# Relative attention: softmax weights turned by 32x32 blocks on VectorE and regrouped through DRAM instead of transposed on TensorE

## The chip, the cores and the metric

The kernel runs on one core of a Trainium2 chip. The metric is the device time of one execution in microseconds. A core has a matrix engine (TensorE, PE in the profile; PEld are its weight loads), VectorE (DVE), ScalarE (ACT), GpSimd (POOL), and SyncE (SP), which here issues the DMAs. Each engine works through its own list of instructions in order and waits on semaphores for the others. Sixteen DMA engines move the data. All data here are float32.

## The reference, cut to what matters

The whole kernel is a sequence of four blocks (relative attention, six layers of local attention and feed-forward, causal attention, a mixture of experts), each followed by a layer norm. The change lies in the first block alone, for 16 batches of 256 tokens, 16 heads of width 8:

```python
q, k, v = (proj(Wq), proj(Wk), proj(Wv))          # [16, 16, 256, 8]
rel = jnp.clip(r[:, None] - r[None, :], -64, 64) + 64
a_q, a_k, a_v = Eq[rel], Ek[rel], Ev[rel]         # [256, 256, 8]
content = jnp.einsum('bhld,bhmd->bhlm', q, k)
rel_k = jnp.einsum('bhld,lmd->bhlm', q, a_k)
rel_q = jnp.einsum('bhmd,lmd->bhlm', k, a_q)
pos_pos = jnp.einsum('lmd,lmd->lm', a_q, a_k)
attn = softmax((content + rel_k + rel_q + pos_pos) / sqrt(8))
out = jnp.einsum('bhlm,bhmd->bhld', attn, v) + jnp.einsum('bhlm,lmd->bhld', attn, a_v)
```

Both products at the end sum over m, the key's position. TensorE sums over partitions, so the weights, which come out of the softmax with l on partitions, are needed with m on partitions.

## The kernel before, in words

**Units.** `relative_attention` treats one batch in eight units: u // 4 chooses the half lc of the queries (128 rows l), the rest of u a group of four heads. A unit is four heads by 128 rows by 256 columns. `weights` (L516) sums the logits in one big PSUM tile, with matmuls for the content and transposes that add the stored position terms `rk3` and `rkc3`; VectorE adds the other term `rq3`, writes the tile `r_lg` and reduces a bound `r_nb` (L558). `exponentials` (L570) makes the weights on ScalarE, in place in `r_lg`. `turn_weights` (L583) transposes the four heads in eight 128x128 transposes on TensorE (L593) into small PSUM tiles, and copies these to `r_pT` (ScalarE L597, VectorE L599), which has m on partitions.

**Use of pT.** When the four units of a half are there, `positions` (L601) multiplies `r_pT` with the relative values (L609, L622), and VectorE masks the result to `r_z` (L630). `values` (L637) multiplies `r_pT` with the projected values in `r_spread` (L645) and gathers `r_z` with `pick` (L656). `join`, `statistics` and `normalise` add the two parts, divide by the sum, add the residual and normalise.

**The position terms.** They are made per batch ahead of time. `turn` and `project` give q and k. `spread_k` (L344) and `shift` (L337) make operands on GpSimd. `rearranged` (L381) sends q or k through DRAM: GpSimd permutes into `r_perm` (L392), four DMAs on SP store it (`there`, L395), four more read it back as `spots` (`r_dk`, `r_dq`), each row to several partitions (`back`, L405, 128 KB each), and `diagonal` masks these on GpSimd (L417). `rq_half`, `rk_half` and the two `corners` steps multiply them with tables of the relative embeddings (L431, L456) and copy or add the results to `rq3` (ScalarE L470, L479), `rk3` (VectorE L490, with the term `pp`) and `rkc3` (VectorE L503).

**Order.** The table `TURNS` (L700) has eight turns for the eight units of a batch; one pass over it is called a batch slot here. An entry (n, step) does the step for the unit n units back, or, for steps that belong to a batch, for the batch n back; -1 is the batch to come. `run` (L771) emits them in this order, and `in_order` (L932) then holds every engine, SP's DMA issues among them, to the order of the program. So a step that waits holds up all that is behind it on its engine. Turn 1, for example, has the exponentials of the unit before, `rearranged` for k of the batch to come, `join`, and the weights of unit 1. Positions for the second half of a batch stand in turn 3 of the next slot, positions for the first half in turn 6.

**Buffers.** Big PSUM tiles: 2. Small ones: 4. `r_lg`: 3; `r_pT`: 2, one for each half.

Of the kernel before, what the change touches and what calls it, by code (L numbers as in the profile page):

```python
# [12 lines left out]
F32 = mybir.dt.float32  # L13
# [4 lines left out]
DRAM = bass.MemoryType.DRAM  # L18

P = 128  # L20
NB, S, D = 16, 256, 128
NT = S // P
H, HD = 16, 8
MAXD = 64
# [80 lines left out]
def bcast(ap, shape):  # L105
    return ap.to_broadcast(list(shape))
# [136 lines left out]
def relative_attention(tc, I, xb, env):  # L243
# [12 lines left out]
    nc = tc.nc  # L256
    V, A, G, T = nc.vector, nc.scalar, nc.gpsimd, nc.tensor
# [7 lines left out]
    with ExitStack() as ctx:  # L265
# [18 lines left out]
        tqc = [one.tile([P, P - 4], F32, name=f"r_tqc{k}") for k in range(2)]  # L284
        tkc = [one.tile([P, P - 4], F32, name=f"r_tkc{k}") for k in range(2)]
        held = ctx.enter_context(tc.tile_pool(name="r_rows", bufs=2, space=DRAM))

        pp = one.tile([P, P], F32, name="r_pp")
        ppc = one.tile([P, MAXD], F32, name="r_ppc")
# [19 lines left out]
        def of(three, b, lc):  # L309
            return three[lc * (1 + b % 2)]  # L310
# [44 lines left out]
        def project_v(b):  # L355

            ps = small()
            for t in range(NT):
                T.matmul(
                    ps[:, t * P : (t + 1) * P],  # L360
                    lhsT=st[b]["xT"][:, t * P : (t + 1) * P],
                    rhs=w["v"],
                    start=True,
                    stop=True,
                )
            v = spread
# [119 lines left out]
        def rk_half(b, s_):  # L486
            for t, l0, n, p_ in diagonals(tk, st[b]["d", "q"], s_):
                pc = pp[:, l0 : l0 + 4 * n].rearrange("p (g i) -> p g i", i=4).unsqueeze(2)
                o = of(rk3, b, t)[:, :, l0 : l0 + 4 * n]
                V.tensor_add(  # L490
                    o.rearrange("p h (g i) -> p g h i", i=4), p_, bcast(pc, (P, n, H, 4))
                )

        def rk_corners(b, phase):

# [14 lines left out]

        def heads(u):

            lc, ap, x = u // 4, u // 2 % 2, u % 2
            return lc, [8 * ap + 4 * k + 2 * x + j for k in range(2) for j in range(2)]

        def weights(b, u):  # L516
# [1 line left out]
            lc, hs = heads(u)  # L518
            s_ = st[b]
            if u % 4 == 0:  # L520
                st[b, lc] = {"den": two.tile([P, H], F32, name="r_den")}
# [24 lines left out]
            for j, h in enumerate(hs):  # L546
# [5 lines left out]
                    start=False,  # L552
                    stop=(j % 2 == 1),
                )
            lg = thr.tile([P, 4, S], F32, name="r_lg")
            nb = thr.tile([P, 4], F32, name="r_nb")
            for j, h in enumerate(hs):
                V.tensor_tensor_reduce(  # L558
# [22 lines left out]
                )  # L581

        def turn_weights(b, u):  # L583
            lc, hs = heads(u)
            lg, _ = st.pop((b, u, "lg"))
            if u % 4 == 0:
                st[b, lc]["pT"] = two.tile([P, 2, H, P], F32, name="r_pT")
            pT = st[b, lc]["pT"]
            h0, x0 = hs[0] // 8 * 8, hs[0] % 4
            for o in range(2):  # L590
                ps = small().rearrange("p (k j s) -> p k j s", k=2, j=2)
                for j in range(4):
                    T.transpose(ps[:, j // 2, j % 2], lg[:, j, o * P : (o + 1) * P], ident)  # L593
                to = pT[:, o, h0 : h0 + 8, :].rearrange("p (k j) s -> p k j s", k=2)
                to = to[:, :, x0 : x0 + 2]
                if o == 0 or u % 2:
                    A.copy(to, ps)  # L597
                else:
                    V.tensor_copy(to, ps)  # L599

        def positions(b, lc):  # L601


            s_ = st[b, lc]
            ps = small()
            for g in range(8):
                for r in range(4):
                    l = 32 * r + 4 * g
                    T.matmul(  # L609
                        ps[32 * r : 32 * r + 32, 64 * g : 64 * g + 64],  # L610
                        lhsT=tv[:, l : l + 4].rearrange("p i d -> p (i d)"),
                        rhs=s_["pT"][:, 0, :, l : l + 4],
                        start=(g == 0),
                        stop=(g == 7 and r // 2 == lc),
                    )
            m = slice(MAXD * lc, MAXD * lc + MAXD)
            for g in range(8):
                for r in range(2):
                    l = 32 * r + 4 * g
                    r_ = r + 2 * (1 - lc)  # L620
                    lr = l + MAXD * (1 - lc)
                    T.matmul(  # L622
                        ps[32 * r_ : 32 * r_ + 32, 64 * g : 64 * g + 64],
                        lhsT=tvc[m, l : l + 4].rearrange("p i d -> p (i d)"),
                        rhs=s_["pT"][m, 1, :, lr : lr + 4],
                        start=False,
                        stop=(g == 7),
                    )
            z = one.tile([P, 8, H, 4], F32, name="r_z")
            V.tensor_mul(  # L630
                z.rearrange("p g h i -> p (g h) i"),
                ps.rearrange("p (a i) -> p a i", i=4),
                bcast(mask4.unsqueeze(1), (P, P, 4)),
            )
            s_["z"] = z

        def values(b, lc):  # L637
# [4 lines left out]
            for q in range(4):  # L642
                for o in range(2):
                    for a in range(4):
                        T.matmul(  # L645
                            po[32 * a : 32 * a + 32, 0:P],
                            lhsT=spread[:, o, lc ^ o, 4 * a + q, :],
                            rhs=s_["pT"][:, o, 4 * a + q, :],
                            start=(q == 0 and o == 0),
                            stop=(q == 3 and o == 1),  # L650
                        )
# [3 lines left out]
            for q in range(4):  # L655
                T.matmul(  # L656
                    pz[:, 0:P],
                    lhsT=pick[:, q, :],
                    rhs=s_["z"].rearrange("p g (a q) i -> p q a g i", q=4)[:, q],
                    start=(q == 0),  # L660
                    stop=(q == 3),
                )
# [27 lines left out]
        def normalise(b, lc):  # L690
# [5 lines left out]

        UNIT = (weights, exponentials, turn_weights)
        TURNS = (  # L700
            (
                (0, spread_k, 1),
                (-1, turn),
                (0, rk_half, 0),
                (0, rk_corners, 0),
                (1, values, 0),
                (2, turn_weights),
                (-1, project),
                (1, exponentials),
                (0, weights),  # L710
            ),
            (
                (1, exponentials),
                (-1, rearranged, "k"),
                (1, join, 0),
                (0, weights),
                (2, turn_weights),
            ),
            (
                (1, exponentials),  # L720
                (0, weights),
                (2, turn_weights),
                (1, statistics, 0),
            ),
            (
                (0, weights),
                (1, positions, 1),
                (1, exponentials),
                (-1, rearranged, "q"),
                (1, values, 1),  # L730
                (2, turn_weights),
            ),
            (
                (-1, diagonal, "k"),
                (1, exponentials),
                (1, join, 1),
                (0, weights),
                (-1, spread_k, 0),
                (-1, rq_half, 0),
                (1, statistics, 1),  # L740
                (2, turn_weights),
            ),
            (
                (-1, rq_corners, 0),
                (0, weights),
                (2, turn_weights),
                (1, exponentials),
                (1, normalise, 1),
            ),
            (  # L750
                (0, project_v),
                (0, weights),
                (-1, rq_half, 1),
                (-1, diagonal, "q"),
                (1, exponentials),
                (0, positions, 0),
                (-1, rk_half, 1),
                (-1, rq_corners, 1),
                (2, turn_weights),
            ),  # L760
            (
                (0, weights),
                (-1, rk_corners, 1),
                (1, normalise, 0),
                (2, turn_weights),
                (1, exponentials),
            ),
        )
        N = NB * NU
# [1270 lines left out]
```

## Time and profile before

| | |
|---|---|
| timed runs, median of 3 | 4094.83 us (4094.47 to 4096.05) |
| profiled execution, span | 4095.9 us |
| relative attention, most of it | from 0 to about 700 us |
| one batch in it | 41.5 us |
| PE, DVE, ACT, POOL busy in the whole span | 98%, 81%, 81%, 68% |
| PE, DVE, ACT, POOL busy from 309.3 to 350.8 us, one batch | 41.23, 28.28, 30.03, 14.96 us |

The span is the time from the first to the last instruction of the one execution that the profiler took; it lies within the timed runs. A busy PE in the table means that some matmul was in flight. A row of a timeline is: start in us, length in us, engine (a name with q is the engine's queue, where DMAs are issued), line, operation, output<-input, count, and in brackets the idle time before it and what ended that. Rows of groups give busy time in us and the mean of one in ns.

### The profile page before, as it was taken

How to read it: one execution, taken by the hardware profiler on the slowest of the kernel's cores; microseconds unless marked ns; L12 is line 12 of the kernel's file. 1: busy time of each engine (PE TensorE's matmuls, PEld its weight loads, DVE VectorE, ACT ScalarE, POOL GpSimd, SP SyncE). 2: the span in 40 equal slices, each digit the busy share in tenths (PEclk: the TensorE clock that was granted, in tenths of full speed). 3: DMA queues.
4: the chain of work that ended last, by engine and by line, in shares of the span. 5: the costliest groups of instructions: out<-in, count | busy, mean ns of one | idle time of the engine just before them, and what ended most of it. 6: DMA issues, size and time to landing. Idle time of an engine off the chain costs nothing.

```text
span 4095.9 us, 141197 instructions
## 1 busy us (share of the span) xinstructions
PE 4006.0 (98%) x57676; PEld 2910.4 (71%) x57676; DVE 3299.3 (81%) x6445; ACT 3298.4 (81%) x11432; POOL 2774.8 (68%) x3334
## 2 busy tenths in 40 slices
PE   8999999899999999999999999999999999989999
PEld 6888887566777677677767767776776777756666
DVE  5666665788888888888888888888888888869985
ACT  4777776688888888888888888888888888879983
POOL 3333332888888888888888888888888888723221
PEclk9999999899999999999999999999999999999999
DMA  2111112100000000000000000000000000000000
GB/s 70 33 35 35 32 37 60 26 16 20 21 24 19 15 20 20 25 21 20 18 26 15 20 20 21 25 19 15 21 15 25 16 15 15 9 4 2 2 8 22
DMA packets 181812, 90.00 MB, mean 22 GB/s; under 512 B 142493, under 2 KB 173220, under 8 KB 181164
## 3 DMA queue, kind: packets, MB, share of 16 engines
q1 hardware_dynamic: 181164, 80.97, 7.5%
q8 instruction: 455, 7.45, 0.8%
q14 instruction: 193, 1.58, 0.1%
HBM read 38.49 MB, written 6.31 MB: 11 GB/s over the span
## 4 chain that ended last, share of the span: by engine, by line
PE 72%; POOL 6%; ACT 3%; issue 2%; DVE 1%; POOLq 0%; DMA 0%; DVEq 0%; ACTq 0%; SPq 0%
PE small L1285 16%; PE big L1135 13%; PE small L1192 8%; PE big L1260 7%; PE big L1207 5%; PE small L1382 3%; PE small L1366 3%; PE small L1350 3%; PE small L1627 3%; POOL a_u L1174 3%; PE big L1583 3%; PE small L1260 2%; PE small L1643 1%; ACT a_g L1268 1%; POOL a_u L1156 1%
## 5 line engine op out<-in xcount | busy, mean ns | idle before, releaser
L1228 ACT ACTIVATE a_pr<-a_pr,a_nb 128x64 f32<-128x64 f32 x3072 | 1024.1, 338 | 5.8 <-DVE a_nb L1221 5.8
L1156 POOL TENSOR_TENSOR a_u<-a_u,a_r 128x1024 f32<-128x1024 f32 x384 | 900.7, 2368 | 30.7 <-DVE a_r L1151 25.6
L1174 POOL TENSOR_TENSOR a_u<-a_u,a_y 128x1024 f32<-128x1024 f32 x384 | 722.5, 1902 | 15.0
L1285 PE MATMUL small<-a_vo,a_g 128*128 128x128 f32 x6144 | 719.0, 275 | 1.6 <-DVE c_st L1500 1.6
L1285 PEld LDWEIGHTS small<-a_vo,a_g 128*128 128x128 f32 x6144 | 702.5, 192 | 2.6 <-ACT a_g L1278 2.5
L1146 ACT ACTIVATE a_sq<-big 128x1024 f32<-128x1024 f32 x384 | 390.9, 1020 | 263.0 <-PE big L1135 262.7
L1228 ACT ACTIVATION_READ_ACCUMULATOR a_pr<-a_pr,a_nb 128x1 f32 x3072 | 587.8, 191 | 0.0
L1192 PEld LDWEIGHTS small<-ident,a_u 128*128 128x128 f32 x3072 | 350.9, 141 | 141.6 <-POOL a_u L1174 90.4
L1163 DVE TENSOR_REDUCE a_ss<-a_sq 128x16 f32<-128x1024 f32 x384 | 445.9, 1201 | 0.0
L1192 PE MATMUL small<-ident,a_u 128*128 128x128 f32 x3072 | 403.0, 274 | 24.5 <-POOL a_u L1174 21.1
L1135 PE MATMUL big<-w_k,a_xs 128*128 128x512 f32 x768 | 382.9, 621 | 4.6 <-ACT a_xs L1075 4.2
L1240 POOL TENSOR_TENSOR a_pr<-a_pr,a_rd 128x1024 f32<-128x1024 f32 x192 | 365.6, 1904 | 13.0 <-DVE a_rd L1239 13.0
L1135 PE MATMUL big<-w_q,a_xs 128*128 128x512 f32 x768 | 362.0, 594 | 0.6 <-DVE a_r L1151 0.6
L1207 PEld LDWEIGHTS big<-a_kT,a_qT 64*32 64x32 f32 x24576 | 262.7, 105 | 123.4 <-issue 63.8
L1215 DVE TENSOR_TENSOR a_pr<-big,w_band 128x1024 f32<-128x1024 f32 x192 | 234.9, 1223 | 108.6 <-PE big L1207 108.6
L1147 DVE TENSOR_TENSOR a_u<-big,a_tak 128x1024 f32<-128x1024 f32 x192 | 235.1, 1225 | 86.9 <-ACT a_sq L1146 86.9
L1207 PE MATMUL big<-a_kT,a_qT 64*32 64x64 f32 x24576 | 294.6, 226 | 4.7 <-POOL a_kT L1185 4.4
L558 DVE CUSTOM_DVE_ANT_0 r_lg<-big,r_rq 128x256 f32<-128x256 f32 x512 | 186.7, 421 | 132.3 <-PE big L547 81.2
L1268 ACT COPY a_g<-big 128x1024 f32<-128x1024 f32 x192 | 193.6, 1008 | 107.0 <-PE small L1260 106.5
L1135 PEld LDWEIGHTS big<-w_q,a_xs 128*128 128x128 f32 x768 | 142.8, 191 | 163.6 <-issue 126.8
L574 ACT ACTIVATE r_lg<-r_lg,r_nb 128x256 f32<-128x256 f32 x512 | 254.6, 511 | 5.0 <-DVE r_nb L558 5.0
L1609 ACT ACTIVATE c_lg<-c_lg,c_nb 128x256 f32<-128x256 f32 x512 | 255.5, 513 | 0.1
(292 smaller groups left out, 9252.8 us busy)
## 6 DMA issues: line engine op xcount, KB each, us to landing
a_xm<-a_xt SPq DMA_DIRECT2D x96, 96.0 KB
r_dk<-r_rowsk SPq DMA_DIRECT2D x64, 128.0 KB
r_dq<-r_rowsq SPq DMA_DIRECT2D x64, 128.0 KB
f_xt<-xa SPq DMA_DIRECT2D x96, 64.0 KB
f_xt<-xa SPq DMA_DIRECT2D x96, 63.5 KB
a_xt<-xa SPq DMA_DIRECT2D x80, 64.0 KB
a_xt<-xa SPq DMA_DIRECT2D x80, 63.5 KB
w_k<-in_L_ffn_Wqkv_dram SPq DMA_DIRECT2D x6, 512.0 KB
```

Of the source, the lines that this page charges most:

```text
L1135: T.matmul(ps[:, c * 512 : (c + 1) * 512], lhsT=xs_of[i, b][:, t, 0:P], rhs=weights[i]["qk"[j]][:, c * 512 : (c + 1) * 512], start=True, s ...
L1146: A.activation(sq, ps3, AF.Square)
L1156: G.tensor_add(u, u, r)
L1163: V.tensor_reduce(ss[:, j], st[m]["sq", j], AX.X, ALU.add)
L1174: G.tensor_mul(u, u, bcast(y[:, j].unsqueeze(2), (P, H, DH)))
L1192: T.transpose(ps[:, k, :], u[:, o : o + P], ident)
L1207: T.matmul(ps[q0 : q0 + WIN, e, c, :], lhsT=qT[DH * e : DH * (e + 1), c, q0 : q0 + WIN], rhs=kT[DH * e : DH * (e + 1), c, t * P + q0 : t * ...
L1228: A.activation(s_["pr"][:, h], s_["pr"][:, h], AF.Exp, bias=s_["nb"][:, h : h + 1], accum_out=s_["den"][:, h : h + 1],)
L1240: G.tensor_mul(s_["pr"], s_["pr"], bcast(rd.unsqueeze(2), (P, H, DH)))
L1260: T.matmul(ps[win], lhsT=x[r, t, :], rhs=pT[r, :, o, :], start=(o == 0), stop=(o == 1),)
L1285: T.matmul(ps[:, 0:D], lhsT=st[m]["g"][:, h, :], rhs=weights[i]["vo"][:, h // 2, h % 2, :], start=(h == 0), stop=(h == H - 1),)
L1609: A.activation(lg[:, j], lg[:, j], AF.Exp, bias=nb[:, j : j + 1], scale=-1.0, accum_out=st[b, lc]["den"][:, h : h + 1],)
```

## The change

`turn_weights` no longer uses TensorE. VectorE turns the four heads of a unit in 32x32 blocks, in one instruction, to a tile `r_ub` that holds a pair of units. After the second unit of a pair, SP issues four DMAs, one for each block of 32 partitions, that write the pair to a DRAM tile with m along the rows (1 MB, in runs of 1 KB). A new step `regroup`, one unit later, has SP read the pair back to `r_pT` (one DMA of 1 MB, in runs of 4 KB); it waits for the four writes. The copies from PSUM (L597, L599) go.

`heads` exchanges the roles of two bits of u, so that a pair of units holds a contiguous half of pT's new layout, and `positions` and `values` address pT and z accordingly. `r_lg` has two buffers instead of three, `r_den` three instead of two.

Work moves between the other engines: in `project_v` the plain copies to `r_spread` go from VectorE to ScalarE; in `rk_half` the half t = 1 is copied by ScalarE without the term `pp`, and a new step `rk_add` adds that term on GpSimd, once for each s_.

In `TURNS`, `turn_weights` (two units back) and `regroup` (three back) come first in every turn. `rk_add` stands in turns 1 and 2, in turn 1 ahead of `rearranged`. `positions` 1 moves to the end of turn 3 and `values` 1 to turn 4; `positions` 0 moves from turn 6 to turn 7; `join`, `statistics` and `normalise` of the second half come one to two turns later.

```diff
         def turn_weights(b, u):
             lg, _ = st.pop((b, u, "lg"))
-            if u % 4 == 0:
-                st[b, lc]["pT"] = two.tile([P, 2, H, P], F32, name="r_pT")
-            pT = st[b, lc]["pT"]
-            h0, x0 = hs[0] // 8 * 8, hs[0] % 4
-            for o in range(2):
-                ps = small().rearrange("p (k j s) -> p k j s", k=2, j=2)
-                for j in range(4):
-                    T.transpose(ps[:, j // 2, j % 2], lg[:, j, o * P : (o + 1) * P], ident)
...
+            if u % 2 == 0:
+                st[b, "ub"] = two.tile([P, 8, 2, P], F32, name="r_ub")
+            ub = st[b, "ub"]
+            V.transpose(
+                ub[:, :, u % 2].rearrange("p w (j q) -> p w j q", q=32),
+                lg.rearrange("p j (w k) -> p w j k", k=32),
+            )
+            if u % 2:
+                o = st[b, u, "rows"] = turned_rows.tile([S, 4, 2 * P], F32, name="r_turned")
+                for a in range(4):
+                    nc.sync.dma_start(
+                        o.rearrange("(w k) a x -> k w a x", k=32)[:, :, a],
+                        ub[32 * a : 32 * a + 32].rearrange("p w c x -> p w (c x)"),
+                    )
+
+        def regroup(b, u):
+            if u % 2 == 0:
+                return
+            lc, x = u // 4, u // 2 % 2
+            if x == 0:
+                st[b, lc]["pT"] = two.tile([P, 2, 2, 4, 8, 32], F32, name="r_pT")
+            nc.sync.dma_start(
+                st[b, lc]["pT"][:, x].rearrange("p o a h q -> p o (a h q)"),
+                st.pop((b, u, "rows")).rearrange("(o p) a x -> p o (a x)", o=2),
+            )
...
-                        V.tensor_copy(o, i)
+                        A.copy(o, i)
...
+                if t:
+                    A.copy(o, p_)
+                else:
+                    V.tensor_add(o, p_, bcast(pc, (P, n, H, 4)))
+
+        def rk_add(b, s_):
+            l = slice(64 * s_, 64 * s_ + 64)
+            o = of(rk3, b, 1)[:, :, l]
+            G.tensor_add(o, o, bcast(pp[:, l].unsqueeze(1), (P, H, 64)))
...
         TURNS = (
             (
+                (2, turn_weights),
+                (3, regroup),
                 (0, spread_k, 1),
                 (-1, turn),
                 (0, rk_half, 0),
                 (0, rk_corners, 0),
                 (1, values, 0),
-                (2, turn_weights),
                 (-1, project),
                 (1, exponentials),
                 (0, weights),
             ),
             (
+                (2, turn_weights),
+                (3, regroup),
                 (1, exponentials),
+                (0, rk_add, 1),
                 (-1, rearranged, "k"),
                 (1, join, 0),
                 (0, weights),
-                (2, turn_weights),
             ),
...
             (
+                (2, turn_weights),
+                (3, regroup),
                 (0, weights),
-                (1, positions, 1),
                 (1, exponentials),
                 (-1, rearranged, "q"),
-                (1, values, 1),
-                (2, turn_weights),
+                (1, positions, 1),
             ),
```

More of the change, by code (lines that the diff above doesn't have):

```diff
@@ L286, in relative_attention @@
         held = ctx.enter_context(tc.tile_pool(name="r_rows", bufs=2, space=DRAM))
+        turned_rows = ctx.enter_context(tc.tile_pool(name="r_turned", bufs=3, space=DRAM))
         pp = one.tile([P, P], F32, name="r_pp")
@@ L489, in rk_half @@
                 o = of(rk3, b, t)[:, :, l0 : l0 + 4 * n]
-                V.tensor_add(
-                    o.rearrange("p h (g i) -> p g h i", i=4), p_, bcast(pc, (P, n, H, 4))
-                )
+                o = o.rearrange("p h (g i) -> p g h i", i=4)
+                if t:
[6 more added lines that the diff above has]
+            G.tensor_add(o, o, bcast(pp[:, l].unsqueeze(1), (P, H, 64)))
         def rk_corners(b, phase):
@@ L511, in heads @@
         def heads(u):
-            lc, ap, x = u // 4, u // 2 % 2, u % 2
+            lc, x, ap = u // 4, u // 2 % 2, u % 2
             return lc, [8 * ap + 4 * k + 2 * x + j for k in range(2) for j in range(2)]
@@ L520, in weights @@
             if u % 4 == 0:
-                st[b, lc] = {"den": two.tile([P, H], F32, name="r_den")}
+                st[b, lc] = {"den": thr.tile([P, H], F32, name="r_den")}
             L = slice(lc * P, (lc + 1) * P)
@@ L554, in weights @@
                 )
-            lg = thr.tile([P, 4, S], F32, name="r_lg")
+            lg = two.tile([P, 4, S], F32, name="r_lg")
             nb = thr.tile([P, 4], F32, name="r_nb")
@@ L583, in turn_weights @@
         def turn_weights(b, u):
-            lc, hs = heads(u)
             lg, _ = st.pop((b, u, "lg"))
-            if u % 4 == 0:
-                st[b, lc]["pT"] = two.tile([P, 2, H, P], F32, name="r_pT")
-            pT = st[b, lc]["pT"]
-            h0, x0 = hs[0] // 8 * 8, hs[0] % 4
-            for o in range(2):
-                ps = small().rearrange("p (k j s) -> p k j s", k=2, j=2)
-                for j in range(4):
[L593 to L599, printed above, removed]
+            if u % 2 == 0:
[22 more added lines that the diff above has]
+            )
         def positions(b, lc):
@@ L611, in positions @@
                         lhsT=tv[:, l : l + 4].rearrange("p i d -> p (i d)"),
-                        rhs=s_["pT"][:, 0, :, l : l + 4],
+                        rhs=s_["pT"][:, :, 0, r, :, 4 * g : 4 * g + 4],
                         start=(g == 0),
@@ L620, in positions @@
                     r_ = r + 2 * (1 - lc)
-                    lr = l + MAXD * (1 - lc)
                     T.matmul(
@@ L624, in positions @@
                         lhsT=tvc[m, l : l + 4].rearrange("p i d -> p (i d)"),
-                        rhs=s_["pT"][m, 1, :, lr : lr + 4],
+                        rhs=s_["pT"][m, :, 1, r_, :, 4 * g : 4 * g + 4],
                         start=False,
@@ L647, in values @@
                             lhsT=spread[:, o, lc ^ o, 4 * a + q, :],
-                            rhs=s_["pT"][:, o, 4 * a + q, :],
+                            rhs=s_["pT"][:, q // 2, o, :, 2 * a + q % 2, :],
                             start=(q == 0 and o == 0),
@@ L658, in values @@
                     lhsT=pick[:, q, :],
-                    rhs=s_["z"].rearrange("p g (a q) i -> p q a g i", q=4)[:, q],
+                    rhs=s_["z"].rearrange("p g (x a j) i -> p x j a g i", x=2, j=2)[:, q // 2, q % 2],
                     start=(q == 0),
@@ L694, in normalise @@
             )
-        UNIT = (weights, exponentials, turn_weights)
+        UNIT = (weights, exponentials, turn_weights, regroup)
         TURNS = (
             (
+                (2, turn_weights),
+                (3, regroup),
                 (0, spread_k, 1),
@@ L716, in relative_attention @@
                 (0, weights),
-                (2, turn_weights),
             ),
             (
+                (2, turn_weights),
+                (3, regroup),
                 (1, exponentials),
+                (0, rk_add, 0),
                 (0, weights),
-                (2, turn_weights),
                 (1, statistics, 0),
@@ L725, in relative_attention @@
             (
+                (2, turn_weights),
+                (3, regroup),
                 (0, weights),
-                (1, positions, 1),
                 (1, exponentials),
                 (-1, rearranged, "q"),
-                (1, values, 1),
-                (2, turn_weights),
-            ),
-            (
+                (1, positions, 1),
+            ),
+            (
+                (2, turn_weights),
+                (3, regroup),
                 (-1, diagonal, "k"),
                 (1, exponentials),
-                (1, join, 1),
+                (1, values, 1),
                 (0, weights),
@@ L739, in relative_attention @@
                 (-1, rq_half, 0),
-                (1, statistics, 1),
-                (2, turn_weights),
-            ),
-            (
+            ),
+            (
+                (2, turn_weights),
+                (3, regroup),
                 (-1, rq_corners, 0),
                 (0, weights),
-                (2, turn_weights),
+                (1, join, 1),
                 (1, exponentials),
-                (1, normalise, 1),
             ),
             (
+                (2, turn_weights),
+                (3, regroup),
                 (0, project_v),
@@ L755, in relative_attention @@
                 (1, exponentials),
-                (0, positions, 0),
+                (1, statistics, 1),
                 (-1, rk_half, 1),
                 (-1, rq_corners, 1),
-                (2, turn_weights),
             ),
             (
+                (2, turn_weights),
+                (3, regroup),
                 (0, weights),
@@ L764, in relative_attention @@
                 (1, normalise, 0),
-                (2, turn_weights),
+                (0, positions, 0),
                 (1, exponentials),
+                (1, normalise, 1),
             ),
```

## The prediction

> **What bounds the kernel now.** I read the busy shares by window first, over one batch of the relative attention. Its pattern recurs every 41.5 us: the four key gathers (L405) are issued at 299.43, 340.89 and 382.74. From 309.3 to 350.8 the columns are the stretch, its length, then busy time (and instructions) of PE, PEld, DVE, ACT and POOL, the granted clock, the share of the DMA engines and GB/s:
>
> ```profile
> 309.30:350.80 41.50, 41.23 (x783) 34.28 (x782) 28.28 (x107) 30.03 (x97) 14.96 (x26) 1.00 0.11 34
> ```
>
> PE never rests, and no other engine exceeds 30 us. Next the groups of this window (busy time, mean ns, idle before), and L1245, the same 32x32 turn in a later stage:
>
> ```profile
> L593 PE MATMUL small<-ident,r_lg 128*128 128x128 f32 x67 | 9.0, 275 | 0.0
> L597 ACT COPY r_pT<-small 128x512 f32<-128x512 f32 x12 | 6.7, 589 | 4.6 <-PE small L593 4.5
> L599 DVE COPY r_pT<-small 128x512 f32<-128x512 f32 x4 | 2.7, 672 | 0.1
> ```
> ```profile
> L1245 DVE STREAM_TRANSPOSE a_pT<-a_pr x192: 1234/1235/1246, 766.2 to 3597.3; 128x1024 f32<-128x1024 f32 x192
> ```
>
> Last the order of time around a turn 1. PE's turn 1 starts with the join (L673); the rows of SP and POOL show the trip of the projected key through DRAM:
>
> ```profile
> 337.76 0.27 PE L673 MATMUL small<-ident,r_oT 128*128 128x128 f32 x1
> ...
> 339.74 1.04 PE L593 MATMUL small<-ident,r_lg 128*128 128x128 f32 x8
> 340.71 0.70 PE L530 MATMUL big<-r_ks,r_q 32*128 32x256 f32 x4
> ```
> ```profile
> 338.30 2.49 SPq L395 DMA_DIRECT2D r_rowsk<-r_perm  x4
> 340.89 2.81 SPq L405 DMA_DIRECT2D r_dk<-r_rowsk  x4
> ```
> ```profile
> 348.69 1.89 POOL L417 TENSOR_TENSOR r_dk<-r_dk,r_mask 128x1024 f32<-128x1024 f32 x1 [1.73 <-DMA r_dk<-r_rowsk]
> ```
>
> So a store group takes SP 2.5 us, a gather group 2.8 us, and the gathered rows are there 7.8 us after the first gather was issued. Two windows say why (the same columns; 670 to 676 holds weight loads over 128 partitions):
>
> ```profile
> 343.00:349.00 6.00, 6.00 (x175) 5.10 (x177) 4.39 (x20) 3.04 (x13) 1.82 (x7) 1.00 0.28 98
> ...
> 670.00:676.00 6.00, 6.00 (x51) 4.69 (x48) 4.42 (x25) 6.00 (x23) 0.86 (x2) 1.00 1.02 337
> ```
>
> The gathers keep the share near a quarter, 4 of 16 engines, each at about 98/4 = 25 GB/s. The loads use all 16.
>
> **What goes.** PE loses eight transposes per unit. From start to the next start (339.74 to 340.71) they take 0.97 us; the eight units of this window add up to 7.5 us. PE falls to 41.5 - 7.5 = 34 us per batch, which is all the change can win. ACT loses 6.7 us (L597) and gains two spread copies (L373's 0.28 each) and half of what L470 takes, 2.25: 26.1. DVE loses L599 (2.7), the spread copies (0.55) and half of L490 (2.7), and gains 8 x 1.235 = 9.9: 31.8. If the new turn's strided blocks cost more than L1245's contiguous ones, the nearest row above is L664 (128x128 from PSUM, 317 ns): 8 x 0.317 = 2.5 per unit, DVE 42; below, as L1245; I take L1245, the same size. POOL gains two additions of 128x1024 as L417, 1.9 each: 18.7, beside 22 us of idle time. Ahead of the key's store the addition delays POOL to about 2.6 us into turn 1; SP gets there only at 5.2 (below), so it costs nothing. The matmuls that read pT take as many columns as before; no row shows their new runs, so: nothing, and the measure after will tell.
>
> By busy time PE would still bound, at 34. But two new things have no row: 1 MB per unit pair written to DRAM in four DMAs, and read back in one. Per batch that is 8 MB: 24.9 us at 337 GB/s, and on the four engines of the gathers 0.5 MB + 0.25 MB at 25 GB/s: 31 us. It fits; order is the matter.
>
> **The trip of pair (6, 7).** Count from PE's start of turn 1.
> - DVE turns unit 7 as its first work of turn 1, behind the reductions of turn 0, which end at 339.53, 1.75 after the start. With 1.24: ready at 3.0.
> - SP issues four writes. The nearest rows: 0.47 us per DMA (L307, xb, also 256 pieces each) to 0.62 (L395). I take 0.57: 5.2.
> - In the same turn SP issues the key's store (2.5) and gathers (first at 7.8, last at 10.6). Only then, in turn 2, comes the read; its wait for the writes is over.
> - Gathered rows land 7.8 us after the first gather: 15.6. The read has a sixteenth of 1 MB, 65 KB, on each engine, and on four of them it is behind the gathers: 65 KB at 25 GB/s is 2.6 us: **18.2**.
>
> PE needs the pair for positions at the end of turn 3. Before it stand the join 0.21 and three weights of 1.83: 5.7 us, 6.4 with the wait for a big buffer, which DVE frees at 4.6. **So PE waits some 12 us.** Behind positions on PE are values, the weights of turn 4 and all that follows; DVE waits too (z of positions is next in its order), and with DVE the next turn.
>
> The rest of the batch is PE's own order, taken from the start times of its matmuls in the timeline from 309.8 to 351.3 (start to next start, transposes left out): positions 2.05; turn 4 5.8 (values 2.88, weights 1.83, a half 1.11), turn 5 2.7, turn 6 5.2, turn 7 4.5, turn 0 7.7. Together 27.95. DVE is near in turn 7 (5.8) and below elsewhere. Period: 18.2 + 27.95 = 46.2.
>
> **The clock** is added. Idle stretches of PE are followed by half clock: of the stretches of one microsecond, those at 0.5 come after 1.7 us or more of idle time. An example:
>
> ```profile
> 737.00:739.00 2.00, 0.40 (x2) 0.40 (x3) 2.00 (x3) 0.02 (x1) 2.00 (x2) 0.64 0.00 0
> 739.00:744.00 5.00, 5.00 (x30) 4.38 (x30) 4.00 (x4) 2.34 (x4) 5.00 (x3) 0.50 0.00 0
> ```
>
> PE works 5 us at half clock, 2.5 us lost. Other places range from 3.4 us (754 to 759) to 13.6 (44 to 58): 1.7 to 6.8 lost. I take 2.5. [...]
>
> The first pairs have a trip too, to positions of the first half at the end of turn 7. Written in turn 5, ready some 1.5 us into it, written by SP 2.3 later, landed 2 later, read back in 3.1 + 2: 10.9, while PE gets there after 10.3; and the query's gathers lie on the four engines ahead. I take 1 us (0 to 3).
>
> **The sum.** 46.2 + 2.5 + 1 = 49.7, 8.2 more than 41.5. Batch slots 1 to 14 have both a store and a gather in turn 1 and positions in turn 3: 14 x 8.2 = 115. Slot 0 has no positions of a batch before: -7.5. Slot 15 has the trip without gathers (5.2 + 2 + 0.5 + 5.1 = 12.8, so 40.8 plus clock 2.5): +2. In the last slot the trip stands bare: +4. Together +113. The profile's span is 4095.9, 1.1 above the median of the timed runs, 4094.83, so I carry the difference over: **4208 us**.
>
> **Rivals.**
> - Lighter: the read is not held behind the gathers. Issued at 10.6, it lands after 0.5 + 3.1 + 2 (the delay from a first gather to moving bytes, 340.89 to about 343): 16.2, or 15 with writes of 0.47 and a shorter delay. Period 43 + 2.5 = 45.5, 14 x 4 - 2 = +54: 4149. The quarter share of the gathers speaks against it. [...]
> - Heavier: the writes are slower than the loads, the pair comes at 21, the clock stays at half for 13.6 us (6.8), and positions of the first half wait 2.5: 21 + 27.95 + 9.3 = 58.3, 14 x 16.8 = +235: 4330.
> - Faster: the trip is hidden and PE runs at its 34 us: 15.6 x -7.5 = -117, 3978. For that the pair must come within 6.4 us of turn 1's start; any gain at all needs 41.5 - 27.95 = 13.5, without loss of clock. SP's own issue after DVE is 2.3 + 2.5 + 2.8 + 0.5 = 8.1, so 11.1 is reached before a byte of the read moves. Only a read or gather much faster than any here, or another order on SP, gets under 13.5.
> - The turns gain nothing because what PE saves equals the wait (arrival at 13 to 14): within 0.2% of now.
>
> **How the numbers follow.** Forecast 58% (4165 to 4290), lighter 14% (4110 to 4165), heavier 13% (4290 to 4380), faster 11%, no difference 4%. A difference under 0.2% (8 us) is about what a measurement of this kernel can't tell from none. The range of 4110 to 4330 leaves out the faster and equal cases (15%) and the upper part of the heavier (5%). Faster 0.11, same 0.04, slower 0.85.
>
> **What would show it.** Right: PE waits at positions (L609 now) once per batch for the DMA that fills r_pT, 8 to 14 us, with PE's share of the stage near 70% and a clock under 1.00; SP's read issued behind r_dk's gathers; the period near 50 us. Wrong: no such wait and a period of 34 to 36 (then the trip was shorter than any row says), a DVE share near all of the period (the turn costs 2.5, not 1.24), or positions and values longer per matmul.

## The result, and the profile after

The changed kernel takes 4393.32 us (median of 4 runs, 4390.72 to 4401.85); the kernel before took 4094.65 us beside it. The ratio is 1.0735, 95% interval 1.072 to 1.075: 299 us slower. The direction was as predicted, but the forecast of 4208 and the range, which ended at 4330, were too low.

The head of the page after shows the span; busy tenths of PE and DVE, PE's clock and the DMA share in 40 slices of 110 us; and the DMA queue:

```profile
span 4388.9 us, 139618 instructions
...
PE   6766667756999999999999999999999999989998
...
DVE  4554555545888888888888888888888888869995
...
PEclk8777788778999999999999999999999999999999
DMA  4565565562000000000000000000000000000000
...
q1 hardware_dynamic: 268204, 215.21, 18.0%
```

The first nine slices are the relative attention. PE was busy for nine tenths and more there, and is now for six or seven; its clock is at seven or eight tenths. From slice twelve on PE and its clock look as before.

The length of a batch slot is read from ACT's copy of the projected q, once per batch. Its first and last start after the setup are 13 slots apart: 87.2 to 626.6 before, **41.5 us** a slot; 94.6 to 872.7 after, **59.9 us**. These are slots 1 to 13: 13 x 18.4 = 239 us of the loss. The setup and slot 0, ahead of them, end 7.4 us later. Slots 14 and 15 and the last positions, behind them, take 134.3 us (872.7 to 1007.0) in the place of 86.5 (626.6 to 713.1), 48 more. Together 294; the two profiled spans differ by 293.

Waits of PE after, from 200 to 700 us (total, times, longest), and one of them in the timeline:

```profile
PE small L631 <- DMA r_pT<-r_turned: 124.0, 8, 16.1
PE big L432 <- DVE r_st L703: 19.6, 8, 2.5
```
```profile
417.58 1.93 PE L631 MATMUL small<-r_pT,r_tv 128*32 128x64 f32 x64 [15.34 <-DMA r_pT<-r_turned]
...
438.27 0.38 PE L432 MATMUL big<-r_dq,r_tk 32*128 32x128 f32 x2 [2.49 <-DVE r_st L703]
```

The first is the predicted wait, once in every slot, at positions of the second half. The second, in turn 6, was not predicted; the profile names `r_st`, VectorE's instruction right behind the reductions that free PE's big tile. SP's queue and POOL show the trip that PE waits for. PE's turn 1 begins at 395.73:

```profile
398.58 3.04 SPq L606 DMA_DIRECT2D r_turned<-r_ub  x4
401.66 3.77 SPq L396 DMA_DIRECT2D r_rowsk<-r_perm  x4
405.54 2.79 SPq L406 DMA_DIRECT2D r_dk<-r_rowsk  x4
408.38 0.44 SPq L618 DMA_DIRECT2D r_pT<-r_turned  x1
408.88 3.20 SPq L606 DMA_DIRECT2D r_turned<-r_ub  x4
```
```profile
415.13 1.89 POOL L418 TENSOR_TENSOR r_dk<-r_dk,r_mask 128x1024 f32<-128x1024 f32 x1 [7.45 <-DMA r_dk<-r_rowsk]
```

The order is the predicted one: writes, key's store, key's gathers, read. The key's rows are there 19.4 us after turn 1's start, the pair 21.9. The next pair's writes are issued half a microsecond behind the read and move beside it. Three windows of the same slot (busy times of PE, PEld, DVE, ACT, POOL, clock, DMA share, GB/s):

```profile
411.00:418.00 7.00, 0.42 (x16) 0.42 (x20) 0.00 (x0) 0.00 (x0) 2.87 (x3) 0.50 0.96 301
418.00:426.00 8.00, 8.00 (x164) 7.02 (x152) 1.84 (x2) 0.27 (x1) 1.65 (x3) 0.55 0.29 79
...
439.00:449.00 10.00, 9.69 (x186) 7.83 (x182) 5.92 (x17) 5.56 (x19) 3.07 (x4) 0.50 0.68 202
```

In the first PE, VectorE and ScalarE stand, GpSimd masks the key's rows, and the DMA engines' share is 0.96. After each of the two idle stretches of this slot PE works for 7 to 10 us at half clock. In slots 1 to 14 it is 3.4 to 8.5 us behind the first stretch; behind the second, which is always 2.4 to 2.5 us long, it is anything from none to 10. Here is one with none, after an idle stretch from 253.74 to 256.19:

```profile
256.20:266.20 10.00, 8.40 (x256) 6.83 (x260) 7.99 (x21) 6.59 (x23) 3.47 (x5) 1.00 0.74 211
```

### The profile page after: what moved, and what is told of

The parts are those of the page before. It is cut to its first block, busy times and chain, and to the rows that moved or that the text cites. A ratio compares the mean times of both kernels' runs of the same rounds, so it can differ in the third digit from the quotient of the medians.

```text
span 4388.9 us, 139618 instructions
## 1 busy us (share of the span) xinstructions
PE 3968.8 (90%) x56652; PEld 2865.1 (65%) x56652; DVE 3354.4 (76%) x6381; ACT 3246.2 (74%) x11368; POOL 2849.7 (65%) x3366
## 4 chain that ended last, share of the span: by engine, by line
PE 72%; POOL 9%; ACT 5%; DMA 5%; issue 5%; DVE 2%; SPq 2%; POOLq 0%; DVEq 0%; ACTq 0%
PE small L1316 15%; PE big L1166 12%; PE small L1223 7%; PE big L1291 7%; PE big L1238 5%; DMA r_pT<-r_turned 4%; PE small L1413 3%; PE small L1397 3%; PE small L1381 3%; POOL a_u L1205 3%; PE small L1658 3%; PE big L1614 3%; PE small L1291 2%; POOL r_rk L500 1%; PE small L1674 1%
## 5 line engine op out<-in xcount | busy, mean ns | idle before, releaser
L1187 POOL TENSOR_TENSOR a_u<-a_u,a_r 128x1024 f32<-128x1024 f32 x384 | 900.5, 2367 | 31.2 <-DVE a_r L1182 26.1
L1205 POOL TENSOR_TENSOR a_u<-a_u,a_y 128x1024 f32<-128x1024 f32 x384 | 722.5, 1902 | 15.0
L1271 POOL TENSOR_TENSOR a_pr<-a_pr,a_rd 128x1024 f32<-128x1024 f32 x192 | 365.6, 1904 | 13.0 <-DVE a_rd L1270 13.0
L631 PE MATMUL small<-r_pT,r_tv 128*32 128x64 f32 x2048 | 54.9, 290 | 263.1 <-DMA r_pT<-r_turned 263.1
```

The source lines that it names most:

```text
L1187: G.tensor_add(u, u, r)
L1205: G.tensor_mul(u, u, bcast(y[:, j].unsqueeze(2), (P, H, DH)))
L1271: G.tensor_mul(s_["pr"], s_["pr"], bcast(rd.unsqueeze(2), (P, H, DH)))
```

## The experiments

All ratios are to the kernel before, with 95% intervals. "Slot" is the mean of 13, read as above.

**Is it the order? e1_late.** Positions of the second half move to the end of turn 6, values to turn 7, join, statistics and normalise to the next slot. (In this kernel and in e8 the second half's values read `r_spread` after the next batch's v has been written there.)

```diff
@@ turn 3
-                (1, positions, 1),
@@ turn 6
+                (1, positions, 1),
@@ turn 7
+                (1, values, 1),
```

> After, with positions of the second half moved from the end of turn 3 to the end of turn 6, its values to turn 7, and its join, statistics and normalise to turns 1, 2 and 3 of the next slot. After has a period of 60 us. Order theory (PE waits 15.5 us at positions because the pair's trip is longer than the way from turn 1 to turn 3, and half clock follows): the wait at positions goes nearly to zero, the period falls to 40 to 44, the time to about 4120 us (4060 to 4180). Load theory (the DMA engines are too busy for 8 MB per batch, wherever the pair is used): the period stays at 50 or more, 4230 us or more.

Measured: 4394.80, 1.0738 (1.072 to 1.0755): no change at all. PE's waits from 200 to 700:

```profile
PE big L432 <- POOL r_dk L418: 62.8, 6, 11.2
...
PE big L432 <- POOL r_dq L418: 20.5, 6, 7.0
```

The wait at positions is gone, and PE waits at the multiplies of the masked rows of k (10.5 us a time; three more such waits, 30.0 us together, are put down to DMAs) and q instead. So there are two chains of about one length, the pair's and the key's, and moving one use gains nothing.

**e2_read_first.** The read stands in turn 1 ahead of the key's store.

```diff
@@ turn 1
-                (3, regroup),
+                (2, regroup),
@@ turn 2
-                (3, regroup),
```

> After, with the read of pair (6, 7) put on SP ahead of the key's store and gathers (regroup two units back in turn 1, none in turn 2). Order theory: the read is issued about 9.5 us into turn 1 instead of 12.7 and lands at 14 instead of 21.9; the wait at positions falls from 15.5 to about 8; the key's gathers come 5 us later and PE waits some 4 us for them ahead of the first rq half; the period falls by 5 to 7 us, the time to about 4300 us (4270 to 4340). Load theory: the same bytes, no change, 4390 us within 30.

Measured: 4398.62, 1.0745 (1.0721 to 1.0768): no change. SP now stops for the writes ahead of the store, and the wait is split (PE, then SP, 200 to 700):

```profile
PE small L631 <- DMA r_pT<-r_turned: 79.4, 17, 9.0
PE big L432 <- POOL r_dq L418: 18.6, 4, 4.9
```
```profile
SPq L618 <- DMA r_turned<-r_ub: 141.0, 43, 9.5
```

**e3_small_gather.** How far do the gathers hold the read?

```diff
+            m = H * 64 if b < 2 else H * 8
...
-                        [[0, 4], [H * 64, HD], [1, H * 64]],
+                        [[0, 4], [H * 64, HD], [1, m]],
```

> After, with the gathers of k and q cut to an eighth of each row from the third batch on (seven eighths of the position terms' columns stay old); as many DMAs as before. Order theory, the part that the four engines of the gathers hold the read: the read lands 5 us sooner after its issue (4 instead of 9.2), the period falls to about 54, the time to about 4310 us. Rival, that the read is slow because the writes of the next pair run beside it on all sixteen engines: the read lands at most 1.5 us sooner, 4370 us or more.

Measured: 4345.91, 1.0616 (1.0595 to 1.0637), 47 less, slot 56.4. The longest wait at positions falls from 16.1 to 13.0 us: the gathers' bytes hold the read by about 3 us. The landing events of the read issued at 408.38 in the changed kernel agree: twelve of its sixteen come by 415.54, the last four at 417.35 to 417.54. The gain is 47 us where about 80 were expected.

**Is it the clock? e4_spin and e4b_spin.** Useless transposes keep PE busy in the wait; the second has more, and some in turn 6.

```diff
+                (1, spin, 112),        # e4b: 140
                 (1, positions, 1),
...
+                (1, spin, 24),         # e4b alone
                 (-1, rk_half, 1),
```

> After, with 112 useless 128x128 transposes of the identity (14.6 us at full clock) on PE ahead of positions of the second half, in the place of its idle time. Clock theory (PE runs about 8 us at half clock behind this wait, 4 us lost per slot): the granted clock stays at 1 from turn 3 into turn 5, the time falls by 14 x 4 = 56 to about 4340 us (4310 to 4365), with more work on PE. Rival (the lower clock comes with the wait but costs nothing): 4390 us or more.

Measured: 4387.44, 1.0718 (1.0696 to 1.0739), a miss: in the slot at 416.76 the 112 took 12.4 us and ended 3.6 us before the pair came, and the clock fell for 6.8 us as soon as work went on.

> As the run with 112 useless transposes, which ended 3.6 us before the pair came, so that the clock still fell; now 140 of them ahead of positions of the second half (15.5 us at 0.11 each) and 24 (2.7 us) ahead of the second rk half in turn 6, where PE is idle for 2.5 us. Clock theory: the granted clock stays near 1 in the whole stage; the lower clock cost 4 us behind the first wait and 5 behind the second, so the period falls from 60 to 51 to 54 and the time to about 4270 us (4230 to 4320). Rival (the period is set by DMA trips, and PE's speed between them doesn't matter): 4370 us or more.

Measured: 4348.76, 1.0624 (1.0603 to 1.0645), 45 less. PE's clock in this kernel, 200 to 700:

```profile
200.00:700.00 500.00, 465.71 (x7792) 402.95 (x7792) 276.23 (x900) 235.63 (x816) 173.59 (x247) 1.00 0.61 174
```

With the clock whole, the slot is 56.7: the clock costs 3.2 us a slot net. I had reckoned 9, half of the 18 us of work at half clock in the slot shown above; the mean of the slots from 200 to 600 is about 13. PE's work bears out the smaller figure: 264.2 us busy in 400 us, or 39.6 a slot, after; here 465.7 in 500, 52.8 a slot, less 164 useless transposes of 0.11 each, 34.8. So the clock lengthens PE's own work by 4.8 us.

**e7_write_order.** The four blocks are written in another order.

```diff
-                for a in range(4):
+                for a in (0, 2, 1, 3):
```

> After, with the four writes of a pair issued in the order of partition blocks 0, 2, 1, 3 instead of 0, 1, 2, 3. In after a pair's writes move at about 190 to 230 GB/s with a DMA share of 0.9, its read at 400. Theory that neighbouring blocks of 32 partitions share the same way out of the memory: writes at 300 GB/s or more, done 1 to 1.5 us sooner, 4350 to 4375 us. Rival (the cost is in pieces of 1 KB): no change, 4390 us within 12.

Measured: 4386.13, 1.0715 (1.0694 to 1.0737), 7 less at most: this order gains little. It is the only other order that was tried, and it still has blocks 2 and 1 side by side.

**The moved additions: e5_rebalance_only and e6_no_rebalance.** The kernel before with them, and the changed kernel without them.

```diff
-                        V.tensor_copy(o, i)
+                        A.copy(o, i)
...
+                (0, rk_add, 1),
                 (-1, rearranged, "k"),
```

> Before, with only the moves between VectorE, ScalarE and GpSimd: spread copies on ScalarE, half t = 1 of rk_half copied by ScalarE, the term pp added by GpSimd in turns 1 and 2. Theory: PE bounds before with 41.2 of 41.5 us per batch, so the moves are worth nothing: 4094 us within 8. Rival (the alternation of ScalarE and VectorE on one PSUM tile makes PE wait for big tiles, as the 2.5 us idle time in turn 6 of after suggests): 4110 us or more.

Measured: 4101.66, 1.0018 (1.0009 to 1.0028), some 8 us.

> The changed kernel with the spread copies and the key's plus addition back on VectorE, nothing on GpSimd. If the moved additions cause PE's second idle stretch (2.5 us in turn 6, then 10 us at half clock): 14 x 5 = 70 less, 4320. If VectorE is only heavier by it: 4380 to 4430.

Measured: 4397.03, 1.0742 (1.0711 to 1.0773): no change, and the wait in turn 6 stays (17.0 us in 7, 200 to 640). The moved additions are neither its cause nor the loss.

**e8_reordered.** All reorderings at once: key's store and gathers ahead of the writes (a step of its own), reads a turn later, positions and values as in e1, write order as in e7.

```diff
@@ turns 1, 3, 5 and 7; send is the four writes
+                (-1, rearranged, "k"),
+                (4, regroup),
+                (2, send),
@@ turn 6
+                (1, positions, 1),
@@ turn 7
+                (1, values, 1),
```

> After, with another order: in turn 1 the key's store and gathers are issued ahead of the writes of pair (6, 7); reads come a turn later, behind the query's gathers (the read of pair (2, 3) stays in turn 6); rq_half 0 moves to turn 5, its corners and the second halves after it; positions of the second half at the end of turn 6, values in turn 7, join in turn 0 of the next slot; writes in the order 0, 2, 1, 3. Order theory (PE waits for the pair or for the key's gathers, whichever trip is the later, since both are queued behind each other): both trips are covered, the period falls to 40 to 46, the time to about 4140 us (4080 to 4210). Load theory (DMA engines busy 0.60 of 60 us, the four of the gathers more): a period of 50 or more, 4240 us or more.

Measured: 4404.01, 1.0756 (1.0738 to 1.0774): no gain. The wait moved once more, to the buffers of turned weights, which the writes still hold (DVE, 200 to 700):

```profile
DVE r_ub L599 <- DMA r_turned<-r_ub: 133.6, 16, 10.8
```

**What does the trip cost at all?** e9 has neither writes nor reads, e11 the writes alone, e10 both. In these, and in e13 to e16, positions and values read a constant.

```diff
-                        rhs=s_["pT"][:, :, 0, r, :, 4 * g : 4 * g + 4],
+                        rhs=bcast(fixed[:, r, :, 4 * g : 4 * g + 4].unsqueeze(1), (P, 2, 8, 4)),
```

> Writes and reads of the pairs are left out, and positions and values read a constant (the embedding windows) in the place of the turned weights; VectorE still turns every unit. If the loss is in the trip through DRAM, the stage falls below the kernel before by what PE saves: 14 slots x 7.5 us = 105 less, 3990 (3960 to 4030). If the turns on VectorE or the moved additions cost time themselves: over 4095.

Measured: 4100.41, 1.0015 (0.9994 to 1.0036), slot 43.1: as long as before, though PE has 7.5 us less to do. (Its four runs spread from 4094 to 4114, and the profile, so the slot, is of the slowest.)

> The writes are made, the reads are left out, and positions and values read a constant. SP then stops for no write, and the gathers share their four DMA engines with no read. If the reads (their wait on SP and their load) hold the key's rows: about 4060 (4010 to 4120). If the writes ahead of the key's store do: over 4250.

Measured: 4220.70, 1.0319 (1.0262 to 1.0375), slot 50.2. Between the two answers: the writes alone cost 7.1 us a slot. (By the medians they cost 120 us in all, by the two profiled runs 97; so 7.1 is rather low.)

> All writes and reads are made, but positions and values read a constant, so nobody waits for a pair. If PE's wait at the positions is the price: at most 4250. If the transfers themselves set the pace (the key's rows come as late as the pair, 19.4 us plus the mask's 2 after the turn): 4370 to 4410, with the wait at the multiplies that read the masked key rows.

Measured: 4321.71, 1.0565 (1.0535 to 1.0596), slot 56.1. Again between: the reads cost 5.9 more although nobody waits for them, and the wait for the pair, net, only the last 3.8 of 59.9. PE's waits of e11 and then of e10, 200 to 700, show where, at the masked rows of k and q:

```profile
PE big L433 <- POOL r_dk L419: 61.0, 10, 7.8
PE big L433 <- POOL r_dq L419: 14.7, 6, 2.8
```
```profile
PE big L433 <- POOL r_dk L419: 63.2, 9, 9.1
PE big L433 <- POOL r_dq L419: 35.3, 8, 7.1
```

**e12_quarter** keeps the trip and its waits, with a quarter of the bytes.

```diff
-                        o.rearrange("(w k) a x -> k w a x", k=32)[:, :, a],
+                        o.rearrange("(w k) a x -> k w a x", k=32)[:, 0:2, a],
...
-                st[b, lc]["pT"][:, x].rearrange("p o a h q -> p o (a h q)"),
+                st[b, lc]["pT"][:, x].rearrange("p o a h q -> p o (a h q)")[:, :, 0:256],
```

> As many writes and reads, in the same order and with the same waits, but a quarter of the bytes in each (two of the eight windows written, 256 of each row's 1024 values read; positions and values read that quarter in the place of all). If bytes set the pace: at most 4250 (the pair at about 16 us after the turn). If the number of transfers, their order and the stops on SP do: 4340 to 4400.

Measured: 4296.55, 1.0504 (1.0473 to 1.0534), slot 54.6; neither answer alone. With a quarter of the bytes the DMA share is 0.23 (200 to 600), and PE still waits 10.3 us a time (200 to 700):

```profile
PE small L633 <- DMA r_pT<-r_turned: 92.8, 9, 11.2
```

So three quarters of the bytes make about 5 of the 15.5 us of that wait; of the 10 that are left the last quarter of the bytes is 1.7 at the same rate, and the rest issue, landing and order (an estimate).

**e14_ready_reads.** Do the reads cost by SP's stops or by their bytes? Here `src` is the input x, always its first 1 MB.

```diff
-                st.pop((b, u, "rows")).rearrange("(o p) a x -> p o (a x)", o=2),
+                bass.AP(src.tensor, src.offset, [[1024, P], [1024 * P, 2], [1, 1024]]),
```

> All writes, and reads of the same size and at the same places, but from the input x, which has long been there, so that SP stops for no write; positions and values read a constant. If the reads cost by SP's stops: about 4225 (as without reads, 4221). If by their bytes beside the gathers and the writes: about 4320 (as with them, 4322).

Measured: 4300.28, 1.0506 (1.0475 to 1.0536), slot 55.8: by far the most is the transfers beside the others; SP's stops are at most about a fifth (21 of 101 us, give or take 18), and in the slots only 0.3 of 5.9.

**What takes the 7.5 us that PE saves?** e13 is e9 without the moved additions; e15 is e9 in the order of before with three `r_lg` buffers; e16 has both, so that it is the kernel before with VectorE's turns and a regrouping that costs nothing.

```diff
@@ e13 and e16
-                        A.copy(o, i)
+                        V.tensor_copy(o, i)
...
-                (0, rk_add, 1),
@@ e15 and e16, each turn as in the kernel before
-            lg = two.tile([P, 4, S], F32, name="r_lg")
+            lg = thr.tile([P, 4, S], F32, name="r_lg")
...
-                (2, turn_weights),
                 (1, exponentials),
...
+                (2, turn_weights),
```

> No writes and no reads (positions and values read a constant), and the moved additions back on VectorE. If the moved additions eat what PE saves: 3990 (3970 to 4030). If not: 4090 to 4140.

Measured: 4092.95, 0.9998 (0.9987 to 1.001), slot 41.5.

> No writes and no reads (positions and values read a constant), the weights in three buffers as before and the steps in the order of the kernel before (each turn of weights at its old place late in the turn, positions and values in turns 3 and 6), with the moved additions kept. If the two buffers and the turns at the head eat what PE saves: 3990 (3970 to 4030). If the work of the other engines does: 4080 to 4110.

Measured: 4124.25, 1.0076 (1.0047 to 1.0105), slot 43.6. PE's waits of e13, then of e15, 200 to 640:

```profile
PE big L433 <- DVE r_st L690: 24.3, 10, 2.4
```
```profile
PE big L433 <- POOL r_dk L419: 25.7, 10, 3.5
```

In the new order the wait is in turn 6: VectorE turns a unit at the head of the turn, ahead of the reductions that free PE's big tile. (The order and the third `r_lg` buffer were changed together, so the runs don't divide the effect between them.) In the old order with the addition on GpSimd ahead of `rearranged`, it is the key's rows. With both the granted clock is lower (means of 0.93 and 0.89 from 200 to 640; 1.00 before, 200 to 600). Each hid the saving alone, which is why neither expectation of a large gain held.

> The kernel before, with only the turns changed: VectorE turns each unit (at the old place, three buffers of weights, the old order, no additions moved), there are no writes and no reads, and positions and values read a constant. If the saving on PE is real and only the new order and the addition on GpSimd hid it: 4010 (3980 to 4040). If other engines or the key's trip hold the slot at 41.5 us: 4080 to 4100.

Measured: 4057.01, 0.9918 (0.9902 to 0.9935), slot 39.1. The window from 200 to 600 of the kernel before, then of e16:

```profile
200.00:600.00 400.00, 397.30 (x7480) 330.31 (x7481) 270.05 (x1026) 286.79 (x930) 143.43 (x252) 1.00 0.11 34
```
```profile
200.00:600.00 400.00, 358.79 (x7329) 288.17 (x7329) 353.82 (x1130) 245.38 (x864) 151.81 (x267) 0.99 0.12 36
```

The saving is real but small: 36 us. VectorE goes from 270 to 354 us busy of 400 and PE waits for it in short stretches, some 40 us together in 200 to 600. The two largest groups:

```profile
PE big L433 <- DVE r_nb L564: 18.3, 16, 1.4
PE big L536 <- DVE r_rk L493: 7.9, 10, 0.8
```

No kernel that makes the trip came below the kernel before.

## Why the prediction was right and where it failed

**Right: the mechanism and its sign.** PE lost its transposes and got one long wait per slot at positions of the second half, for the DMA that fills `r_pT`; the chain is turn, four writes, key's store, key's gathers, read, in SP's order; half clock follows, for 3.4 to 8.5 us of PE's work. The wait is 15.5 us, though, where 8 to 14 were named as the sign. VectorE's turn is 1.24 us (L599), as taken from L1245, and the pair is turned at 2.8 us (3.0 predicted).

**Failed: the period of 49.7 us, a sum along one chain.** It is 59.9. The terms:

| term | predicted | measured |
|---|---|---|
| trip of the pair, to its landing | 18.2 | 21.9 |
| rest of PE's order | 27.95 | about 31 |
| wait in turn 6 | 0 | 2.5 |
| clock | 2.5 | 4.8 |
| positions of the first half | 1 | 0 |

The measured terms are those of the slot that starts at 395.73, except the clock's, which is from e4b. "About 31" is what is left of 59.9; up to 1 us of it is clock too, since PE is busy 40.6 us in this slot and 39.6 in the mean. It agrees with two other readings: PE's work without transposes came to 34.8 (e4b) and 35.0 (e16: 358.79 of 400, times 39.06) a slot rather than 34, and PE's short waits for VectorE and ScalarE add some 2 us.

- *The trip.* Four writes took SP 3.0 us (2.3 predicted), the store 3.8 (2.5). The gathers' rows came 9.6 us after their first issue rather than 7.8, and the read 9.2 us after its own. I took durations from a trace without pair transfers; here pair writes lie beside store, gathers and read. A pair whose trip is free of them, in turn 5 (430.72 to 441.98), is back 11.3 us after its first write, where my terms for such a pair were 2.3 + 2 + 5.1 = 9.4, and its read lands 4.9 us after its issue. The "shorter delay" of the lighter rival had no row, and no run shows it: this read's 4.9 stand against 5.1 in my terms.
- *Turn 6.* I costed the new places in `TURNS` for what they add and not for what they stand ahead of on VectorE. The turn went ahead of the reductions, with two `r_lg` buffers, and PE's big tile came free 2.5 us later.
- *The clock.* Two idle stretches per slot instead of one. The row after one of them is 10 us of busy PE at 0.50, where I had taken 5; behind the first stretch half clock lasted 3.4 to 8.5 us of PE's work, behind the second from none to 10. e4b gives the price, 3.2 us a slot.

**Failed: the terms of the ends.** "Slot 0: -7.5" went the other way: from copy to copy of the projected q it takes 50.9 us, 41.1 before. With no pair to wait for at turn 3, PE comes upon the key's rows (PE's waits, 43.7 to 95):

```profile
PE big L432 <- POOL r_dk L418: 7.7, 1, 7.7
PE small L631 <- DMA r_pT<-r_turned: 3.6, 1, 3.6
```

The 48 us behind the last copy hold slot 14 (+8.2 forecast), slot 15 (+2) and the last positions (+4). From PE's turn 1 of slot 14 to that of slot 15 it is 57.7 us (40.7 before), from there to the next turn 1 58.1 (39.9), from there to the last positions 16.9 (4.3): 17, 18 and 13 more. In slot 15 not only the trip itself counts. SP's queue in slot 15:

```profile
934.92 3.04 SPq L606 DMA_DIRECT2D r_turned<-r_ub  x4
942.52 0.70 SPq L1068 DMA_DIRECT2D a_xt<-xb  x1
943.26 0.79 SPq L1069 DMA_DIRECT2D a_xt<-xb  x1
944.10 2.76 SPq L1070 DMA_DIRECT2D a_xt<-xb  x1
946.96 0.52 SPq L165 DMA_DIRECT2D w_k<-in_L_ffn_Wqkv_dram  x1
947.67 0.38 SPq L618 DMA_DIRECT2D r_pT<-r_turned  x1
```

The next block's loads stand between writes and read, where the key's transfers stood in other slots, and PE waits 15.7 us again. After that, with no weights left to sum, two more pairs are waited for in full (11.8 and 14.9 us).

**Failed: "PE falls to 34 us per batch, which is all the change can win".** With the trip free (e16) the slot is 39.1 and the gain 36 us, not 117; VectorE, which I had at 31.8 of 34 in the changed kernel (the terms listed there add up to 32.2), has 34.5 of 39.1 there (without the moved additions), and PE waits for it. So the faster rival, 3978, could not have come about by a fast trip alone: with the change's own order and additions, and no trip, the time is that of before (e9).

**One chain was not the whole.** I wrote that any gain needs the pair within 13.5 us, as though all else were clear. The key's rows, gathered behind the same writes, come late as well. The steps from e16 to the changed kernel, per slot: 39.1 with turns alone; 41.5 with the new order (e13); 43.1 with the moved additions (e9); 50.2 with the writes (e11); 56.1 with the reads (e10); 59.9 when positions wait for the pair. Only the last 3.8 is what the wait adds, though the profile writes 15.5 us on that line. The steps hold the clock too: PE is busy 35.0 us a slot in e16, 38.7 in e11 and 42.4 in e10 (301.94 of 400, times 56.13), with as much to do. The step from e13 to e9 is 7 us in all by the medians, so about 0.6 a slot rather than 1.6.

**Open.** Bytes and order share the cost of the trip (e3, e12, e14), but the runs don't divide the writes' 7.1 us between time on SP and time in the DMA engines. Whether a second issuing queue would help was not tried.

## What to carry to other kernels

A wait that the profile puts on one line is worth only the distance to the next chain (here 3.8 of 15.5 us): before pricing its removal, look for the second transfer that hangs on the same queue, and test by a kernel in which the data are constant. When an engine gives work away, find what the others do with the time: here freeing 7.5 of PE's 41.5 us was worth 2.4 in the best order that was run: the receiving engine filled up (VectorE, from 270 to 354 us of 400), and PE got short waits for it. Price a DMA by rows in which its new neighbours move too, and count everything that its queue issues in the same stretch, other layers' loads included.

## What was not expected of the hardware

- Writing a pair (1 MB from blocks of 32 partitions, in runs of 1 KB) moves 183 to 264 GB/s at a DMA share of 0.86 to 0.94 (windows of 1 us, 432 to 436 and 444 to 448), where reads in runs of 4 KB move 385 to 426 (439 to 441, 451 to 453).
- Issuing the four DMAs of the key's store took SP 2.5 us before (2.8 once) and 3.8 to 4.2 in the changed kernel. The query's store took 2.5 to 3.8 before and 5.7 to 6.9, with a read and a pair's writes in flight; part of this is waiting for the read to land (14.2 us in eight slots, 200 to 700).
- An addition of 128x1024 on GpSimd takes 2.37 us, with a broadcast operand (L500) as without (L1187 of the next block); multiplications of that size by a broadcast operand take 1.89 to 1.90 (L418, L1205, L1271). The prediction had priced the addition at 1.9.
- PE idle for only 2.5 us was followed by half clock in 12 slots of 14, for 3 to 10 us; 3.6 us (e4) by 6.8.
